# LSTM recurrence with a filled-in second layer: ScalarE's filler work by a budget, x's clamp on VectorE, the output sum through PSUM

## Chip, cores and metric

One core of a Trainium2 chip. The metric is the device time of one execution in microseconds, the median of several runs. Every engine (TensorE or PE, VectorE or DVE, ScalarE or ACT, GpSimd or POOL, SyncE or SP) works through its own queue in order; semaphores order them among each other.

## The reference

`x` has 8 sequences of 512 steps with 512 features, `cond` is 8 x 512. Two residual layers follow each other.

```python
# layer 1: an LSTM, hidden size 512, started from cond
a = x_t @ Wx + b + h @ Wh                  # 2048 columns
i, f, o = sigmoid(a[:, :1536]) in thirds;  g = tanh(a[:, 1536:])
c = f * c + i * g;   h = o * tanh(c)
x = x + h                                  # for all t
# layer 2: a causal convolution over 8 taps (cond holds the taps), then a scan over 64 states
conv = conv_b + sum_k x_pad[:, k:k+512] * cond[k]
proj = conv @ Wp + bp                      # 128 columns
B = softplus(proj[:, :64]);  C = tanh(proj[:, 64:]);  u = x @ Ws + bs
s = decay * s + dt * B * u;  y = C * s
x = x + y @ Wo + bo
```

All in fp32 at the interface.

## The kernel before

The features lie on the partitions in four chunks k = 0 to 3 of 128, time and batch on the free axis (8 batch columns per step). Layer 1 is a loop over 512 steps written out in full. Layer 2 is cut into blocks of 32 steps (256 columns), at the end into 32, 16, 8 and 8; its work is put into the gaps of the loop as *filler*.

**One recurrent step.** The hidden units are worked in two halves, A and B, each with its own PSUM tiles. Both matrices are held as a high and a low fp16 part. Per step and half (letters are those of the string `ORDER`, lines those of the profile before):

- PE: `h_mm` (L317) multiplies the state `stat` of the step before into the PSUM tile `hp` of the half, in the order A0 A1 b0 A2 A3 B1 B2 B3 and at `H` the last 64 columns of half B; `x_mm` (L306) adds the input's product for a step pair ahead. PE needs the state of half A for chunks 0 and 1, of half B for 2 and 3.
- VectorE: `T` and `t` transpose `hp` (L577, L580), `a` adds the halves of the gates into `zp` (L584), `v` and `c` update the cell, `c` into `zp` columns 48 to 63 (L599, L603), `i`, `m` and `l` make the new state (L612, L615, L618).
- GpSimd: `b` (L589). ScalarE: `g`, `o`, `k` (L593, L596, L606) are the tanh's, `p` (L609) copies the cell, `y` (L673) preloads a PSUM tile with the bias, `q` (L668) is a small copy.

`zp` is a pair of PSUM tiles, one per half, 64 columns each.

**Filler.** `Filler` holds a list per kind of work, and `pop` takes the head of a list if its dependencies were done at least a step (`gap`) before. While the loop is written out, three places in each step take from these lists:

- at `H`, behind the last x matmuls of the step, PE takes from `pl2`, `pl` until a budget is used up (1 unit, from step 480 on 3; a matmul of 128 columns is a unit);
- at `f`, behind the last state update, VectorE takes from `xd`, `d2`, `dve` as long as the told costs fit into `FILL` = 0.8;
- at `E`, at the end of the step, ScalarE takes two entries from `xa`, `al2`, `al`, and GpSimd one from `po`.

An entry can be several instructions: `act1` is two ScalarE instructions (L515, L516), `act2` four (the three of `softplus_act`, L206 to L208, and L520). What is left when the loop ends is drained list by list; that is the tail. Before it stand 14 dummy matmuls (L622).

**The filler by line.** For the input of layer 1 (`add_x`, per block and chunk): clamp on GpSimd (L441), fp16 high part on ScalarE (L444), low part on VectorE (L446). For a block of layer 2 (`add_l1`): the copy of the 7 steps before the block (L471, ScalarE); x + h per chunk (L476, VectorE); convolution, first tap on ScalarE (L493), seven on VectorE (L488); the matmul for u (L500) and ScalarE's bias (L502); the projection (L509); `act1`, `act2`; on VectorE softplus (L212 to L218), dt * B * u (L531), carry (L533), scan (L535), carry out (L537), C * s (L538); the output matmul of each chunk (L544) into a bank of `fps`, and VectorE's sum of it with the bias and x (L548), then the store. In the last three blocks one to four chunks of the convolution go to PE (`wpj`, L509).

The PSUM tiles are `hpb` (four of 512 columns), `fps` (two of 512) and the two `zp`.

Of the kernel before, what the change touches and what calls it, by code (L numbers as in the profile page):

```python
# [9 lines left out]
F32 = mybir.dt.float32  # L10
I32 = mybir.dt.int32
AF = mybir.ActivationFunctionType
# [14 lines left out]
DUMMY = 4  # L27
FILL = 0.8
TAILD = 14
LN2 = 0.6931471805599453  # L30
# [4 lines left out]
class Filler:  # L35
# [5 lines left out]
    def __init__(self, banks):  # L41
        self.q = {q: [] for q in ("po", "xa", "xd", "pl2", "d2", "al2", "pl", "dve", "al", "sp")}
        self.done = {}
        self.n = 0
        self.banks = banks
        self.free = {i: -10 for i in range(len(banks))}
# [34 lines left out]

    def drain(self, engs=("po", "xa", "xd", "al2", "d2", "d2", "d2", "pl2", "pl2", "pl", "pl", "dve", "al", "sp"),
              upto=None):

        def more(e):
            return self.q[e] and (upto is None or self.q[e][0][0] <= upto)
        while any([more(e) and self._try(e, None) for e in engs]):
            pass
# [3 lines left out]
def lstm_conv_ssm_kernel(ctx: ExitStack, tc: tile.TileContext, xT, condT, wx, wh, brow, cbp, wpp, bpp,  # L92
# [5 lines left out]
    l1blocks = [(i * BLK, BLK, 0) for i in range(NBLK - 2)]  # L98
    l1blocks += [(T - 64, 32, 0), (T - 32, 16, 4), (T - 16, 8, 4), (T - 8, 8, 2)]
    v, s, pe, sp = nc.vector, nc.scalar, nc.tensor, nc.sync  # L100
# [66 lines left out]

    zp = [pp.tile([128, 64], F32, name=f"zp{i}") for i in range(2)]
    fps = [pp.tile([128, 2 * NT], F32, name=f"fps{i}") for i in range(2)]
# [34 lines left out]
    def softplus_act(a, e, x):  # L204

        s.activation(e, a, AF.Exp, scale=-1.0)  # L206
        s.activation(a, a, AF.Tanh, scale=0.5, bias=hln2[0:64])
        s.activation(x, a, AF.Square, scale=-0.5, bias=half[0:64])  # L208

# [17 lines left out]
    s.activation(sp2[0], al2, AF.Abs)  # L227
    softplus_act(*sp2[0:3])
    dt = sp2[3][:, 1:2]
# [136 lines left out]


    bsum = [cp.tile([128, 256], F32, name=f"bsum{h}") for h in range(2)]
    run(*first[:4])
# [56 lines left out]
    for k in range(4):  # L426
        last = fl.add("pl", lambda k=k: pe.matmul(bk0["b"][:, 0:1], wp[:, k], cb[:, k:k + 1], start=k == 0, stop=k == 3),
                      take=bk0 if k == 0 else None)
    fl.add("al", lambda: s.activation(bpc, bk0["b"][:, 0:1], AF.Identity, bias=bp), deps=(last,), gap=0, give=bk0)
    for k in range(4):  # L430
        for j in range(8):
            fl.add("al", lambda k=k, j=j: s.activation(wpj[:, j, k], wp[:, k], AF.Copy, scale=cond[:, k, j:j + 1]))

# [3 lines left out]
    def add_x(n, t0=0, after=-1):  # L437
        for k in range(4):
            src, tmp, dst = x_parts(n, k, t0)
            sx = SX[:, k:k + 1]  # L440
            a = fl.add("po", lambda k=k, src=src, tmp=tmp: nc.gpsimd.tensor_scalar(  # L441
                tmp, src, CL[:, 0, k:k + 1], CL[:, 1, k:k + 1], op0=ALU.min, op1=ALU.max),
                deps=(xlast.get((n - 1, k)),), after=after)
            a = fl.add("xa", lambda sx=sx, tmp=tmp, dst=dst: s.activation(dst[0], tmp, AF.Copy, scale=sx),  # L444
                       deps=(a,), after=after)
            xlast[n, k] = fl.add("xd", lambda sx=sx, tmp=tmp, dst=dst: v.scalar_tensor_tensor(  # L446
                dst[1], tmp, sx, dst[0], op0=ALU.mult, op1=ALU.subtract), deps=(a,), after=after, cost=0.4)
# [4 lines left out]
    def add_l1(i, t0, L, pk):  # L452
# [11 lines left out]
        unit, cost = max(N / 128, 1), N / 1000 + 0.14  # L464
        kk = 1

# [3 lines left out]
        if i:  # L470
            halo = fl.add("al", lambda: s.activation(X[:, :, 0:H0], Xp[:, :, Lp * NB:Lp * NB + H0], AF.Copy),  # L471
                          deps=(p1["x2"], free), after=A)
        x2 = []
        for k in range(0, 4, kk):
            def f(k=k):
                v.scalar_tensor_tensor(X[:, k:k + kk, H0:H0 + N],  # L476
                                       hb[n % 2][:, k:k + kk, r0:r0 + L, :].rearrange("p k t b -> p k (t b)"), 0.5,
                                       xbuf[n % 4][:, k:k + kk, r0 * NB:r0 * NB + N], op0=ALU.mult, op1=ALU.add)
            x2 += [fl.add("dve", f, deps=(free,), after=A, cost=kk * cost)] * kk
        me["x2"] = x2[-1]  # L480

        cvd = {}
        for j in range(8):
            for k in range(pk, 4):
                def f(k=k, j=j):
                    src = X[:, k, j * NB:j * NB + N]
                    if j:
                        v.scalar_tensor_tensor(cv[:, k, 0:N], src, cond[:, k, j:j + 1], cv[:, k, 0:N],  # L488
                                               op0=ALU.mult, op1=ALU.add)
                    elif pk:  # L490
                        s.activation(cv[:, k, 0:N], src, AF.Copy, scale=cond[:, k, 0:1])  # L491
                    else:
                        s.activation(cv[:, k, 0:N], src, AF.Identity, bias=cb[:, k:k + 1], scale=cond[:, k, 0:1])  # L493
                deps = (halo, x2[k], p1.get("proj")) if j == 0 else (cvd[k],) if j == 1 else ()
                cvd[k] = fl.add("dve" if j else "al", f, after=A, deps=deps, cost=cost)

        bk = {}
        for k in range(4):
            def f(k=k, bk=bk):
                pe.matmul(bk["b"][0:64, 0:N], ws[:, k], X[:, k, H0:H0 + N], start=k == 0, stop=k == 3)  # L500
            last = fl.add("pl", f, deps=(x2[k], p2.get("u")), after=A, take=bk if k == 0 else None, cost=unit)
        fl.add("al", lambda bk=bk: s.activation(u[:, 0:N], bk["b"][0:64, 0:N], AF.Identity, bias=bs),  # L502
               deps=(last,), gap=0, give=bk)
        bk = {}
# [8 lines left out]

        def act1(bk=bk):
            s.activation(ab[:, 0:N], bk["b"][0:64, 0:N], AF.Abs, bias=b[0:64])  # L515
            s.activation(rl[:, 0:N], bk["b"][0:64, 0:N], AF.Relu, bias=b[0:64])  # L516

        def act2(bk=bk):
            softplus_act(ab[:, 0:N], e[:, 0:N], x[:, 0:N])
            s.activation(C[:, 0:N], bk["b"][64:128, 0:N], AF.Tanh, bias=b[64:128])  # L520
        last = fl.add("al2", act1, deps=(last, p2.get("wo")), gap=0)
        last = fl.add("al2", act2, deps=(last, p1.get("y")), give=bk)
        for f in softplus_dve(ab[:, 0:N], e[:, 0:N], x[:, 0:N], rl[:, 0:N], w[:, 0:N]):
            fl.add("d2", f, deps=(last,), cost=cost)

# [3 lines left out]
        def bt(a):  # L529
            return a[:, 0:N].rearrange("p (b t) -> p t b", b=NB)  # L530
        me["u"] = fl.add("d2", lambda: v.scalar_tensor_tensor(bt(e), tb(rl), dt, tb(u), op0=ALU.mult, op1=ALU.mult),  # L531
                         cost=cost)
        fl.add("d2", lambda: v.scalar_tensor_tensor(bt(e)[:, 0], carry, dec, bt(e)[:, 0],  # L533
                                                    op0=ALU.mult, op1=ALU.add), cost=0.18)
        fl.add("d2", lambda: v.tensor_tensor_scan(w[:, 0:N], dect[L].rearrange("p b t -> p (b t)"), e[:, 0:N], 0.0,  # L535
                                                  op0=ALU.mult, op1=ALU.add), cost=1.6 * cost)
        fl.add("d2", lambda: v.tensor_copy(carry, bt(w)[:, L - 1]), cost=0.1)  # L537
        me["y"] = y = fl.add("d2", lambda: v.tensor_tensor(tb(C), tb(C), bt(w), op=ALU.mult), cost=1.3 * cost)  # L538
        kb = min(2 * NT // N, 4)
        for k0 in range(0, 4, kb):  # L540
            bk = {}
            for k in range(k0, k0 + kb):
                def f(k=k, bk=bk):
                    pe.matmul(bk["b"][:, k % kb * N:k % kb * N + N], wo[:, k], C[:, 0:N], start=True, stop=True)  # L544
                me["wo"] = last = fl.add("pl2", f, deps=(y,), take=None if k % kb else bk, cost=unit)
            for k in range(k0, k0 + kb):
                def g(k=k, bk=bk):
                    v.scalar_tensor_tensor(o[:, k, 0:N], bk["b"][:, k % kb * N:k % kb * N + N], bo[:, k:k + 1],  # L548
                                           X[:, k, H0:H0 + N], op0=ALU.add, op1=ALU.add)
                me["out"] = fl.add("d2", g, deps=(last,), gap=0, give=bk if k == k0 + kb - 1 else None, cost=cost)  # L550
        fl.add("sp", lambda: sp.dma_start(outT[:, :, t0:t0 + L, :].rearrange("p k t b -> p k (t b)"), o[:, :, 0:N]),
# [76 lines left out]
    for t in range(T):  # L628
# [17 lines left out]
        for op in ORDER.split():  # L646
# [11 lines left out]
            elif op == "f":  # L658
                left = FILL
                while True:  # L660
                    got = fl.pop("xd", t, left) or fl.pop("d2", t, left) or fl.pop("dve", t, left)
                    left -= got
                    if not got:
                        break
# [17 lines left out]
            elif op == "E":  # L682
                for _ in range(2):
                    fl.pop("xa", t) or fl.pop("al2", t) or fl.pop("al", t)
                fl.pop("po", t)
            else:
                getattr(ch[op[1]], "o_" if op[0] == "o" else op[0])()
# [5 lines left out]

    fl.drain(("al2", "d2", "d2", "d2", "pl", "pl", "dve", "al"))
    fl.drain()
# [62 lines left out]
```

## Time and profile before

| | us |
|---|---|
| runs (3) | 1887.14 to 1888.98, median 1888.84 |
| profiled execution | 1887.91 |
| its span on the core | 1886.1 |
| first L577 of step 0, from the span's start | 42.41 |
| first L577 of step 511 | 1848.68 |
| VectorE busy | 1661.7 (88%) |
| PE busy | 1614.8 (86%) |
| ScalarE busy | 913.4 (48%) |

Granted clock of PE over the span: 0.992.

Rows of the operations that the change touches, mean of one in ns (busiest shape):

| line | engine | shape | count | mean |
|---|---|---|---|---|
| L441 clamp | POOL | 128x256 | 60 | 592 |
| L444 high part | ACT | 128x256 | 60 | 500 |
| L446 low part | DVE | 128x256 | 60 | 476 |
| L493 first tap | ACT | 128x256 | 60 | 589 |
| L488 other taps | DVE | 128x256 | 420 | 477 |
| L476 x + h | DVE | 128x256 | 60 | 417 |
| L548 last sum | DVE | 128x256 | 60 | 474 |
| L544 output matmul | PE | 64x256 | 120 records, two a matmul | 425 |
| L673 bias into PSUM | ACT | 128x256 | 508 | 383 |

How to read the views: in the timeline a row is start, duration (both us), engine, line, operation, out<-in, and in brackets the idle time of the engine before it with what ended it; neighbours of a kind are merged. In the waits a row is who waited for whom, the sum in us, how often, and the longest.

### The profile page before, as it was taken

What the parts mean: (1) busy time and instruction counts of PE and PEld (TensorE: products, weight loads), DVE (VectorE), ACT (ScalarE), POOL (GpSimd) and SP (SyncE); (2) the same over time, 40 slices, a digit from 0 to 9 for tenths busy, and PEclk for the clock granted to TensorE, in tenths of its full rate; (3) what the DMA queues carried; (4) which work ended last, traced back from release to release, by engine and by line L of the source; (5) the groups of instructions that cost most, each with busy time, mean ns of one, the idle gap of its engine ahead of it and who ended that gap; (6) DMA issues with size and microseconds to landing.
All of it is one profiled execution on the core that took longest, in us unless ns stands there. A gap on an engine that the chain in (4) does not pass through costs nothing.

```text
span 1886.1 us, 123963 instructions
## 1 busy us (share of the span) xinstructions
PE 1614.8 (86%) x53917; PEld 1313.1 (70%) x53917; DVE 1661.7 (88%) x9392; ACT 913.4 (48%) x5194; POOL 316.0 (17%) x1366
## 2 busy tenths in 40 slices
PE   5878888888888889888888988889888888988897
PEld 4666676677677677776776767767766767767686
DVE  8878889898998989889898998989899898998985
ACT  5555444454544545444454544445444454544442
POOL 1211111111211111111121111111111121111110
PEclk8999999999999999999999999999999999999997
DMA  6000000000000000000000000000000000000000
GB/s 238 5 4 15 4 27 4 4 27 4 27 4 4 27 4 27 4 27 4 4 27 4 26 5 4 27 5 27 4 27 5 4 15 4 16 4 15 5 5 23
DMA packets 21444, 33.78 MB, mean 18 GB/s; under 512 B 2592, under 2 KB 19616, under 8 KB 19872
## 3 DMA queue, kind: packets, MB, share of 16 engines
q1 hardware_dynamic: 20656, 25.71, 4.0%
q8 instruction: 421, 6.90, 1.5%
q14 instruction: 127, 1.04, 0.2%
q10 hardware_dynamic: 240, 0.13, 0.0%
HBM read 17.45 MB, written 8.39 MB: 14 GB/s over the span
## 4 chain that ended last, share of the span: by engine, by line
DVE 67%; PE 16%; ACT 7%; issue 4%; POOL 4%; DMA 1%; SPq 0%; DVEq 0%; ACTq 0%
DVE Z L577 18%; PE hp L317 13%; DVE Zo L580 9%; DVE wraw L488 9%; DVE zp L584 8%; DVE stat L618 4%; POOL zo L589 4%; DVE stat L612 4%; ACT gate L596 4%; DVE u L599 3%; DVE zp L603 3%; DVE hb L615 3%; ACT tc L606 2%; DMA x<-in_xT_dram 1%; PE fps L509 1%
## 5 line engine op out<-in xcount | busy, mean ns | idle before, releaser
L317 PE MATMUL hp<-whh,stat 128*16 128x256 f16 x18428 | 1017.8, 262 | 239.9 <-DVE stat L618 225.9
L317 PEld LDWEIGHTS <-stat 128*16 128x16 f16 x36856 | 860.0, 92 | 486.7 <-DVE stat L618 408.6
L317 PE MATMUL hp<-whl,stat 128*16 128x256 f16 x18428 | 1013.3, 261 | 0.2 <-DVE whl L281 0.2
L593 ACT ACTIVATE gate<-zp 128x48 f32<-128x48 f32 x1022 | 214.8, 210 | 781.5 <-DVE zp L584 778.9
L306 PE MATMUL hp<-wxh,xs 128*32 128x256 f16 x8192 | 518.4, 273 | 6.4 <-DVE xs L357 6.4
L306 PE MATMUL hp<-wxl,xs 128*32 128x256 f16 x8192 | 518.8, 273 | 0.0
L577 DVE STREAM_TRANSPOSE Z<-hp 128x192 f32<-128x192 f32 x1024 | 391.6, 382 | 102.0 <-PE hp L317 89.9
L589 POOL TENSOR_TENSOR zo<-Zo 128x16 f32<-128x16 f32 x1024 | 226.4, 221 | 1455.0 <-DVE Zo L580 1455.0
L306 PEld LDWEIGHTS <-xs 128*32 128x32 f16 x16384 | 403.5, 97 | 15.8 <-DVE xs L357 6.7
L596 ACT ACTIVATE gate<-zo 128x16 f32<-128x16 f32 x1022 | 220.9, 216 | 141.2 <-POOL zo L589 140.9
L612 DVE SCALAR_TENSOR_TENSOR stat<-gate,tc 128x16 f16<-128x16 f32 x1024 | 178.4, 174 | 68.5 <-ACT tc L606 0.2
L580 DVE STREAM_TRANSPOSE Zo<-hp 128x64 f32<-128x64 f32 x1024 | 233.3, 228 | 2.7
L584 DVE TENSOR_TENSOR zp<-Z 128x48 f32<-128x48 f32 x1024 | 211.6, 207 | 0.0
L618 DVE TENSOR_TENSOR stat<-hb,stat 128x16 f16<-128x16 f32 x1024 | 186.8, 182 | 17.5
L673 ACT ACTIVATE hp<-bsum 128x256 f32<-128x256 f32 x508 | 194.7, 383 | 0.0
L488 DVE SCALAR_TENSOR_TENSOR wraw<-x2b,cond,wraw 128x256 f32<-128x256 f32 (+1 forms) x434 | 188.5, 471 | 4.7 <-ACT wraw L491 4.7
L609 ACT ACTIVATE gate<-zp 128x16 f32<-128x16 f32 x1024 | 189.5, 185 | 0.0
L615 DVE SCALAR_TENSOR_TENSOR hb<-gate,tc 128x16 f32<-128x16 f32 x1024 | 187.2, 183 | 0.0
L606 ACT ACTIVATE tc<-zp 128x16 f32<-128x16 f32 x1024 | 185.0, 181 | 0.2 <-DVE zp L603 0.2
L599 DVE SCALAR_TENSOR_TENSOR u<-gate 128x32 f32<-128x32 f32 x1024 | 175.7, 172 | 4.5 <-ACT gate L593 3.7
L603 DVE SCALAR_TENSOR_TENSOR zp<-u 128x16 f32<-128x16 f32 x1024 | 177.4, 173 | 0.0
L681 POOL COPY seenp<-gate 128x1 f32<-128x1 f32 x256 | 46.9, 183 | 79.5 <-ACT gate L596 79.5
(125 smaller groups left out, 774.7 us busy)
## 6 DMA issues: line engine op xcount, KB each, us to landing
x<-in_xT_dram SPq DMA_DIRECT2D x15, 512.0 KB, 4.0
out_dram<-wraw SPq DMA_DIRECT2D x15, 512.0 KB, 3.6
wraw<-in_wh_dram SPq DMA_DIRECT2D x4, 1024.0 KB, 14.4
wraw<-in_wx_dram SPq DMA_DIRECT2D x4, 1024.0 KB, 11.2
x<-in_xT_dram SPq DMA_DIRECT2D x2, 256.0 KB, 13.3
wp<-in_wp_dram SPq DMA_DIRECT2D x1, 256.0 KB, 7.0
out_dram<-wraw SPq DMA_DIRECT2D x1, 256.0 KB, 2.8
out_dram<-wraw SPq DMA_DIRECT2D x2, 128.0 KB, 2.2
```

The costliest lines, as they stand in the source:

```text
L306: pe.matmul(hp[h][P % 2][32 * q:32 * q + 32, :], S[:, k, P % (BLK // 2)], W[:, k, q, 256 * h:256 * h + 256], start=False, stop=False, tile ...
L317: pe.matmul(hp[h][(t // 2) % 2][32 * q:32 * q + o + 16, a], S[:, k, 0:o + 16], wb[0][p][:, k, q, 256 * h + a.start:256 * h + a.stop], star ...
L488: v.scalar_tensor_tensor(cv[:, k, 0:N], src, cond[:, k, j:j + 1], cv[:, k, 0:N], op0=ALU.mult, op1=ALU.add)
L577: v.transpose(self.Z.rearrange("p g r -> p (g r)"), self.P[:, 0:192])
L580: v.transpose(self.Zo.rearrange("p g r -> p (g r)"), self.P[:, 192:256])
L584: v.tensor_tensor(self.zp[:, 0:48].rearrange("p (g b) -> p g b", b=8), self.Z[:, :, o:o + 8], self.Z[:, :, o + 8:o + 16], op=ALU.add)
L589: pool.tensor_tensor(self.zo.rearrange("p (g b) -> p g b", b=8), self.Zo[:, :, o:o + 8], self.Zo[:, :, o + 8:o + 16], op=ALU.add)
L596: s.activation(self.G[:, 48:64], self.zo, AF.Tanh, scale=self.inv)
L603: v.scalar_tensor_tensor(self.zp[:, 48:64], self.u[:, 1], 0.5, self.u[:, 0], op0=ALU.mult, op1=ALU.add)
L612: v.scalar_tensor_tensor(self.S[:, :, 0:8], r8(self.G[:, 48:64]), 1.0, r8(self.tc), op0=ALU.add, op1=ALU.mult)
L615: v.scalar_tensor_tensor(self.hf, r8(self.G[:, 48:64]), 1.0, r8(self.tc), op0=ALU.add, op1=ALU.mult)
L618: v.tensor_tensor(self.S[:, :, 8:16], self.hf, self.S[:, :, 0:8], op=ALU.subtract)
```

## The change

- Clamp of x: from GpSimd (`po`) to VectorE (`xc`), taken at `f`.
- x + h of a block: a list of its own (`x2`), which `f` asks before the clamp and before layer 2's other VectorE work.
- ScalarE at `E`: no longer two entries, but as many as fit by their told costs into `FILLA` = 1.0. `act1` and `act2` are split into single instructions (the tanh of C now third), each with a cost. GpSimd gets no filler any more.
- The told costs of VectorE's strided or scanned pieces are raised (1.7 and 1.6 times `cost`), that of the first softplus piece is lowered.
- For blocks of 32 steps the output no longer goes through `fps`. The two `zp` tiles become 512 columns wide, the recurrence keeps columns 0 to 63, and columns 64 to 319 are `ops`. ScalarE writes x + bias there (L561), PE adds the output product (L566, accumulating), ScalarE copies the sum to SBUF (L572). All on the list `ao`, two chunks at a time. The shorter blocks keep the old way (L550, L554).
- Two matmuls of 512 columns in the prologue write both `zp` banks once.
- The block of steps 448 to 479 takes one chunk of its convolution on PE.

In the changed kernel the recurrence's L584, L603, L618 are L607, L626, L641.

```diff
+FILLA = 1.0
...
-    l1blocks += [(T - 64, 32, 0), (T - 32, 16, 4), (T - 16, 8, 4), (T - 8, 8, 2)]
+    l1blocks += [(T - 64, 32, 1), (T - 32, 16, 4), (T - 16, 8, 4), (T - 8, 8, 2)]
...
-    zp = [pp.tile([128, 64], F32, name=f"zp{i}") for i in range(2)]
+    zps = [pp.tile([128, 512], F32, name=f"zp{i}") for i in range(2)]
+    zp = [t[:, 0:64] for t in zps]
+    ops = [t[:, 64:64 + NT] for t in zps]
...
+    for b_ in zps:
+        pe.matmul(b_, ident, x2b[0].rearrange("p k n -> p (k n)")[:, 0:512], start=True, stop=True)
...
-            a = fl.add("po", lambda k=k, src=src, tmp=tmp: nc.gpsimd.tensor_scalar(
+            a = fl.add("xc", lambda k=k, src=src, tmp=tmp: v.tensor_scalar(
                 tmp, src, CL[:, 0, k:k + 1], CL[:, 1, k:k + 1], op0=ALU.min, op1=ALU.max),
-                deps=(xlast.get((n - 1, k)),), after=after)
+                deps=(xlast.get((n - 1, k)),), after=after, cost=0.27)
...
+        acost = N / 1000 + 0.24
...
-            x2 += [fl.add("dve", f, deps=(free,), after=A, cost=kk * cost)] * kk
+            x2 += [fl.add("x2", f, deps=(free,), after=A, cost=cost + 0.06)]
...
-        last = fl.add("al2", act1, deps=(last, p2.get("wo")), gap=0)
-        last = fl.add("al2", act2, deps=(last, p1.get("y")), give=bk)
-        for f in softplus_dve(ab[:, 0:N], e[:, 0:N], x[:, 0:N], rl[:, 0:N], w[:, 0:N]):
-            fl.add("d2", f, deps=(last,), cost=cost)
+        acts = [lambda bk=bk: s.activation(ab[:, 0:N], bk["b"][0:64, 0:N], AF.Abs, bias=b[0:64]),
+                lambda bk=bk: s.activation(rl[:, 0:N], bk["b"][0:64, 0:N], AF.Relu, bias=b[0:64]),
+                lambda bk=bk: s.activation(C[:, 0:N], bk["b"][64:128, 0:N], AF.Tanh, bias=b[64:128])]
+        acts += softplus_act(ab[:, 0:N], e[:, 0:N], x[:, 0:N])
+        for m, f in enumerate(acts):
+            last = fl.add("al2", f, deps=(last, (p2.get("wo"), None, None, p1.get("y"), None, None)[m]), gap=0,
+                          give=bk if m == 2 else None, cost=acost)
...
+            for k in range(k0, k0 + kb):
+                def g(k=k, bk=bk):
+                    s.activation(ops[k % 2], X[:, k, H0:H0 + N], AF.Identity,
+                                 bias=bo[:, k:k + 1])
+                pre = fl.add("ao", g, deps=(me.get("out", p1.get("out")), x2[k]), after=A, cost=acost)
             for k in range(k0, k0 + kb):
                 def f(k=k, bk=bk):
-                    pe.matmul(bk["b"][:, k % kb * N:k % kb * N + N], wo[:, k], C[:, 0:N], start=True, stop=True)
-                me["wo"] = last = fl.add("pl2", f, deps=(y,), take=None if k % kb else bk, cost=unit)
+                    pe.matmul(ops[k % 2], wo[:, k], C[:, 0:N], start=False,
+                              stop=False, skip_group_check=True)
+                me["wo"] = last = fl.add("pl2", f, deps=(y, pre), gap=1, cost=unit)
+
             for k in range(k0, k0 + kb):
-                def g(k=k, bk=bk):
-                    v.scalar_tensor_tensor(o[:, k, 0:N], bk["b"][:, k % kb * N:k % kb * N + N], bo[:, k:k + 1],
-                                           X[:, k, H0:H0 + N], op0=ALU.add, op1=ALU.add)
-                me["out"] = fl.add("d2", g, deps=(last,), gap=0, give=bk if k == k0 + kb - 1 else None, cost=cost)
+                def h(k=k):
+                    s.activation(o[:, k, 0:N], ops[k % 2], AF.Copy)
+                me["out"] = fl.add("ao", h, deps=(last,), cost=acost)
...
-                    got = fl.pop("xd", t, left) or fl.pop("d2", t, left) or fl.pop("dve", t, left)
+                    got = (fl.pop("xd", t, left) or fl.pop("x2", t, left) or fl.pop("xc", t, left) or fl.pop("d2", t, left)
+                           or fl.pop("dve", t, left))
...
-                for _ in range(2):
-                    fl.pop("xa", t) or fl.pop("al2", t) or fl.pop("al", t)
-                fl.pop("po", t)
+                left = FILLA
+                while True:
+                    got = fl.pop("xa", t, left) or fl.pop("ao", t, left) or fl.pop("al2", t, left) or fl.pop("al", t, left)
+                    left -= got
+                    if not got:
+                        break
```

## The prediction

> **What bounds the kernel now.** I read the page first (shares and chain), then the timeline of a plain recurrence step and of one with a filler that hurts, then the waits, then the timeline of the tail.
>
> ```profile
> PE 1614.8 (86%) x53917; PEld 1313.1 (70%) x53917; DVE 1661.7 (88%) x9392; ACT 913.4 (48%) x5194; POOL 316.0 (17%) x1366
> DVE 67%; PE 16%; ACT 7%; issue 4%; POOL 4%; DMA 1%; SPq 0%; DVEq 0%; ACTq 0%
> ```
>
> No engine is full; a chain that runs once per step through PE, VectorE and ScalarE sets the pace. The timeline shows one plain step (first transpose L577 at 1059.26, next at 1062.76) and most of the next one:
>
> ```profile
> 1059.26 0.38 DVE L577 STREAM_TRANSPOSE Z<-hp 128x192 f32<-128x192 f32 x1
> ...
> 1060.33 0.22 DVE L584 TENSOR_TENSOR zp<-Z 128x48 f32<-128x48 f32 x1
> ...
> 1060.46 0.18 DVE L603 SCALAR_TENSOR_TENSOR zp<-u 128x16 f32<-128x16 f32 x1
> ...
> 1060.73 0.70 PE L544 MATMUL fps<-wraw,wo 64*128 64x256 f32 x2
> ...
> 1061.25 0.17 DVE L618 TENSOR_TENSOR stat<-hb,stat 128x16 f16<-128x16 f32 x1
> ...
> 1062.76 0.38 DVE L577 STREAM_TRANSPOSE Z<-hp 128x192 f32<-128x192 f32 x1
> ...
> 1065.17 0.59 POOL L441 TENSOR_SCALAR xc<-x,cl 128x256 f32<-128x256 f32 x1
> ...
> 1065.36 0.42 DVE L618 TENSOR_TENSOR stat<-hb,stat 128x16 f16<-128x16 f32 x1
> ```
>
> Call the start of the first L577 of a step 0. Half B's gate sum L584 starts at 1.07, half A's cell update L603 at 1.20, and a filler matmul of the output projection (L544) runs on PE from 1.47 to 2.17, after all recurrent work of PE in that step and before the next. L618 of half A starts at 1.99 and frees PE for the next step; 3.50 after the start comes the next L577. So the stretch from 1.07 to 1.99 on VectorE is on the chain with no slack, and L544 beside it costs nothing: nobody in that stretch waits for it.
>
> From the starts of the first L577 (42.41 for step 0, 1848.68 for step 511) 511 intervals make 1806.27 us. Steps with nothing but recurrence, and most with two fillers, take 3.498. The excess over that is 1806.27 - 511 x 3.498 = 18.8 us. It is 14.0 in blocks 1 to 14 (1.0 each), 1.3 in the first 32 steps and 3.4 in the last 31. Inside a block it sits in few steps: four with a clamp on POOL (L618 takes 0.42 instead of 0.17 while L441 runs, as shown; +0.25, +0.06, +0.25, +0.06), the one behind the four-in-one ScalarE piece (+0.29), and one with L218 and L531 together on VectorE, 1.09 us (+0.15, 0.09 given back).
>
> **The parts, costed.**
>
> *Clamp to VectorE, ScalarE by budget.* 64 POOL clamps go; 64 VectorE ones come. Nearest rows: L212, the same kind of operation on 64 rows by 256, 0.277 us; POOL's own 0.592. I take 0.28. In the built order each stands with L476 (0.417) or L446 (0.476): 0.70 to 0.76. Two L488 (0.477 each, 0.95) fit today at 3.498, so this hides. At 0.592 it would make 1.07 and cost about 0.15 in four steps per block, 9 us. ScalarE gets at most two long pieces per step or three of 0.393, 1.18 us at the dearest. Today a pair of L493 (0.589 each) starts at 1065.48 and ends 1066.56, 0.06 after the next L577 and 0.37 before the L584 starts whose output ScalarE needs first, so these hide; without that cover each tenth over 0.37 would be a tenth on the step. The POOL, four-in-one and L531 excesses go: the 14.0 us, and about 1.0 of the first block. In the last 31 steps the excess comes from two or three PE fillers in one step (two of 256 columns +0.31, three of 128 columns +0.12). The built order has 5 and 7 such steps there, 2.4 in place of 3.4. **Gain: 14.0 + 1.0 + 1.0 = 16.0 us.**
>
> *Last sum through PSUM.* 60 L548 (0.474) leave VectorE's fillers, worth nothing on the chain; 60 + 60 ScalarE pieces come. Their bounds are L673 (0.383, into PSUM) and L493 (0.589, with a bias); even two at 0.589 hide as above. The matter is where the sums live: in columns 64 to 319 of the same two tiles whose columns 0 to 63 are zp, the recurrence's own buffers. The waits of the built program follow the tile, not the columns. All 56 matmuls (L566) that stand inside the loop keep L544's place on PE, behind the last x matmul of the step, and VectorE's next write of that half's zp waits for the matmul: for half A that is the cell update (L603, now L626), for half B the gate sum (L584, now L607). Both stand ahead of everything else VectorE has in the step.
>
> The price, from the shown rows: PE ends at 2.17, and VectorE starts 0.04 after PE's end (in the tail PE ends L544 at 1876.40, L548 starts at 1876.44), so at 2.21. Half B: 2.21 - 1.07 = 1.14 late. Half A: 2.21 - 1.20 = 1.01 late. Everything to L618 queues behind; PE waits for L618; so the whole step grows by it. 26 steps of each: 26 x 2.15 = 55.9. Two more steps hold two L566 each; two L544 in one step took 1.13 us, so half B's sum starts at 1.47 + 1.13 + 0.04 = 2.64, 1.57 late: 3.1. **Cost: 59.0 us.** Bounds per wait: 0.8, if VectorE's pieces close up behind it, to 1.3, if the second wait that the instruction now carries and the restart add 0.15; 45 to 73 in all.
>
> Could such a wait be empty, because the columns differ? The waits of the kernel before show the same kind biting: PE's matmul into the last 64 columns of a half's hp tile waits for the transpose that reads the first 192.
>
> ```profile
> PE hp L317 <- DVE Z L577: 1.0, 2, 0.5
> ```
>
> The Trainium skill, PSUM — Partial Sum Buffer, "PSUM bank collisions raise a hardware error", goes further: accesses are to be guarded by bank and quadrant, never by address. By that rule every L566 has to wait for zp's users and they for it, and the sum keeps the 59.0; by columns alone it would be nil. No run here shows such a collision.
>
> *The start.* Two matmuls of 512 columns on fp32 now stand on PE between L327 (9.85 + 0.37) and L339 (10.95). L292's 256 columns take 12.05/48 = 0.25 per record, two records a matmul: 0.5, so 1.0 for 512 columns, 2.0 for both. L339 then starts near 12.2 rather than 10.95. Behind it are the bias matmuls, ScalarE's bsum and its first L276, from which ScalarE and VectorE run chained to step 0. **Cost 1.2 us** (0 to 1.5).
>
> *The tail.* VectorE's and ScalarE's second-layer work now comes later in a block, and the end feels it.
>
> ```profile
> 1851.09 0.35 ACT L515 ACTIVATE wraw<-fps,bpc 64x128 f32<-64x128 f32 x1
> ...
> 1853.20 7.36 PE L509 MATMUL fps<-x2b,wraw 128*128 128x64 f32 x64
> ...
> 1868.52 0.31 ACT L515 ACTIVATE wraw<-fps,bpc 64x64 f32<-64x64 f32 x1 [5.62 <-PE fps L509]
> ...
> 1882.04 0.86 DVE L548 SCALAR_TENSOR_TENSOR wraw<-fps,bo,x2b 128x64 f32<-128x64 f32 x4 [2.06 <-PE fps L544]
> ```
>
> From the last step's L577 (1848.68) the first of these is at +2.4 and the end of the last at +34.2. In the built order ten of the 32 projection matmuls of the 16-step block are left behind the dummies: 2.4 + 1.7 + 10 x 0.29 = +7.0 for its first activation. The next block's 32 matmuls need a bank that ScalarE frees at +8.1, and end at 8.1 + 7.4 = +15.5 (now +11.9). Then four L566 with a hand-over to ScalarE and back between pairs (about 3.1) and the 16-step block's four (2.0): +20.6. The last block's projection is split around the output matmuls of the block before it; these wait for that block's y. VectorE turns to it when the 16-step block's sums (1.2) and the last ScalarE piece behind them are through, near +22.5, and needs 3.3 for eleven pieces and the convolution pieces between: +25.8. Then two outputs 1.0, two projections 0.5, two outputs 1.0, nine 2.1 and two 1.0 on PE: +31.4. Behind that, as now: six activations 1.6, VectorE's eleven pieces 2.8, four matmuls 2.0, four sums 0.9, 0.1 of hand-overs = +38.8. **Cost 4.6 us** (2 to 8).
>
> *Sum.* 59.0 - 16.0 + 1.2 + 4.6 = +48.8 on the profiled execution's 1887.91 (span 1886.1 and 1.8 around it): 1936.7. The median of the runs is 0.9 above that execution, so **1937.6**.
>
> **Rivals.**
> 1. The waits don't bite: L566 is done before VectorE comes to zp. Then the gain stands alone, 1888.8 - 16.0 + 5.8 = 1878.6, faster. It needs L566 to end before 1.07, against 2.17 in the trace; the break-even is (16.0 - 5.8)/56 = 0.18 us per wait. For it speaks only that ends of matmuls are modelled; but L548's start behind L544 fits them within 0.04. 5%.
> 2. Only one half's waits reach the end, say because half A's delay is taken up by pieces that otherwise wait for half B: 1937.6 - 26 x 1.01 = 1911. Against it: L618 of half A itself lies behind L603. 6%.
> 3. ScalarE's new pieces come late as well: L584 of half A also waits for ScalarE's last access to zp in four steps per block. If that ended 0.2 after 0.43, 56 x 0.2 = 11 more: 1949. By the rows it ends 0.4 or more before. 9%.
>
> **How the numbers follow.** The forecast has 80%. Its own bounds are 1937.6 - 14 - 3 to 1937.6 + 14 + 3, and up to 9 more for a dear clamp; rival 3 lies inside, rival 2 outside. 1919 to 1955 should hold 8 in 10. A difference under 0.2% (3.8 us) can't be told from none here. Faster 0.05 (rival 1), same 0.01, slower 0.94.
>
> **What would show it.** Right: steps 14, 15, 18 and 19 of a block at 4.5 to 4.7 us with VectorE idle about 1 us, released by PE's L566; all other steps of blocks 1 to 14 at 3.50; L618 nowhere at 0.42; first L577 near 43.6; last span after it near 42. Wrong: these four steps at 3.5, or VectorE idle before other work than L607 and L626.

## The result, and the profile after

The changed kernel takes **1939.88 us** (median of 4 runs, 1939.44 to 1940.68) against 1888.64 for the kernel before on the same chip: ratio 1.0277, 95% interval 1.0264 to 1.029. It is slower by 2.8%. The profiled execution took 1939.63, its span is 1937.9.

In the changed kernel the lines that the prediction speaks of are L600 (first transpose), L607 (gate sum), L626 (cell update), L641 (state, low part), L566 (output matmul into `ops`), L561 and L572 (ScalarE before and behind it), L448 (clamp) and L373 (the two initial matmuls). From the page, busy times and the chain that ended last:

```profile
PE 1615.7 (83%) x53935; PEld 1318.0 (68%) x53935; DVE 1656.2 (85%) x9389; ACT 954.4 (49%) x5313; POOL 281.8 (15%) x1302
DVE 62%; PE 26%; ACT 5%; issue 4%; POOL 3%; DVEq 0%; POOLq 0%; ACTq 0%
```

PE has 1 us more work than before and VectorE 5.5 us less, yet the span is 51.7 longer: the chain's share moved from VectorE (67 to 62%) to PE (16 to 26%). The timeline shows two neighbouring steps of a block; the columns are start, duration, instruction, and in brackets the idle time before it and what ended that.

```profile
1015.72 0.38 DVE L600 STREAM_TRANSPOSE Z<-hp 128x192 f32<-128x192 f32 x1 [0.21 <-PE hp L321]
...
1017.19 0.70 PE L566 MATMUL zp<-wraw,wo 64*128 64x256 f32 x2
1017.93 0.18 DVE L626 SCALAR_TENSOR_TENSOR zp<-u 128x16 f32<-128x16 f32 x1 [0.92 <-PE zp L566]
...
1018.68 0.17 DVE L641 TENSOR_TENSOR stat<-hb,stat 128x16 f16<-128x16 f32 x1
...
1020.19 0.38 DVE L600 STREAM_TRANSPOSE Z<-hp 128x192 f32<-128x192 f32 x1
...
1021.67 0.70 PE L566 MATMUL zp<-wraw,wo 64*128 64x256 f32 x2
1022.41 0.22 DVE L607 TENSOR_TENSOR zp<-Z 128x48 f32<-128x48 f32 x1 [1.11 <-PE zp L566]
...
1023.32 0.17 DVE L641 TENSOR_TENSOR stat<-hb,stat 128x16 f16<-128x16 f32 x1
...
1024.82 0.38 DVE L600 STREAM_TRANSPOSE Z<-hp 128x192 f32<-128x192 f32 x1
```

The first step is 1020.19 - 1015.72 = 4.47 long, the second 1024.82 - 1020.19 = 4.63, where a plain step takes 3.498. In both the matmul keeps its old place (it starts 1.47 and 1.48 after the step's start and takes 0.70), and VectorE stands idle 0.92 and 1.11 before the very instructions that write that half's zp. L641 of half A comes 2.96 and 3.13 after the step's start instead of 1.99. The waits (engine and line that waited, what it waited for: us in total, times, longest) count them:

```profile
DVE zp L607 <- PE zp L566: 31.7, 28, 1.5
DVE zp L626 <- PE zp L566: 23.8, 26, 0.9
ACT tc L629 <- DVE zp L626: 22.3, 26, 0.9
```

In the kernel before, VectorE's writes of zp wait for no matmul. All kernels below are taken apart in the same way: the start of step 0 (first transpose), the 511 intervals between first transposes, their excess over 511 x 3.498, and the rest of the span (tail). "With" are the steps in which an output matmul into `ops` starts. All from the profiled executions, in us.

| kernel | start | 511 steps | excess | of it with / without | tail | span |
|---|---|---|---|---|---|---|
| before | 42.4 | 1806.3 | 18.8 | | 37.5 | 1886.1 |
| after | 44.9 | 1849.9 | 62.4 | 58.2 / 4.3 | 43.0 | 1937.9 |
| e1_old_sum | 42.0 | 1792.6 | 5.1 | | 50.3 | 1884.9 |
| e2_only_sum | 44.8 | 1868.2 | 80.7 | 61.8 / 18.9 | 47.1 | 1960.0 |
| e4_late_one_tile | 44.9 | 1799.9 | 12.4 | 8.1 / 4.3 | 47.0 | 1891.7 |
| e5_init_late | 42.0 | 1850.4 | 62.9 | | 42.7 | 1935.0 |
| e6_one_chunk_pe | 42.3 | 1794.7 | 7.2 | | 43.5 | 1880.5 |
| e7_own_bank | 42.3 | 1791.8 | 4.4 | 0.7 / 3.6 | 55.3 | 1889.5 |
| e8_pool_clamp | 41.5 | 1803.6 | 16.1 | | 49.4 | 1894.5 |
| e9_bank_chunk | 42.3 | 1792.0 | 4.6 | | 49.6 | 1883.9 |
| e10_last_old | 42.3 | 1792.5 | 5.1 | | 34.4 | 1869.2 |

The runs of e2, e7 and e9 fall in two groups 6 to 8 us apart, and their profiled executions (1961.78, 1891.28 and 1885.71) are of the longer group, so that their spans here are 5 to 7 us longer than their median run's.

### The profile page after: what moved, and what is told of

It is laid out like the page before. It is cut to its first block, busy times and chain, and to the rows that moved or that the text cites. A ratio compares the mean times of both kernels' runs of the same rounds, so it can differ in the third digit from the quotient of the medians.

```text
span 1937.9 us, 124180 instructions
## 1 busy us (share of the span) xinstructions
PE 1615.7 (83%) x53935; PEld 1318.0 (68%) x53935; DVE 1656.2 (85%) x9389; ACT 954.4 (49%) x5313; POOL 281.8 (15%) x1302
## 4 chain that ended last, share of the span: by engine, by line
DVE 62%; PE 26%; ACT 5%; issue 4%; POOL 3%; DVEq 0%; POOLq 0%; ACTq 0%
PE hp L321 19%; DVE Z L600 17%; DVE Zo L603 8%; DVE zp L607 7%; DVE wraw L495 6%; DVE stat L641 4%; DVE zp L626 4%; DVE stat L635 3%; DVE u L622 3%; POOL zo L612 3%; PE hp L310 3%; ACT gate L619 3%; DVE hb L638 3%; PE zp L566 2%; ACT tc L629 1%
## 5 line engine op out<-in xcount | busy, mean ns | idle before, releaser
L600 DVE STREAM_TRANSPOSE Z<-hp 128x192 f32<-128x192 f32 x1024 | 392.4, 383 | 101.1 <-PE hp L321 88.1
L607 DVE TENSOR_TENSOR zp<-Z 128x48 f32<-128x48 f32 x1024 | 212.5, 207 | 31.7 <-PE zp L566 31.7
L603 DVE STREAM_TRANSPOSE Zo<-hp 128x64 f32<-128x64 f32 x1024 | 233.3, 228 | 2.1
L626 DVE SCALAR_TENSOR_TENSOR zp<-u 128x16 f32<-128x16 f32 x1024 | 177.3, 173 | 23.8 <-PE zp L566 23.8
L641 DVE TENSOR_TENSOR stat<-hb,stat 128x16 f16<-128x16 f32 x1024 | 179.0, 175 | 17.5
L495 DVE SCALAR_TENSOR_TENSOR wraw<-x2b,cond,wraw 128x256 f32<-128x256 f32 (+1 forms) x427 | 184.8, 471 | 0.0
```

The costliest lines, as they stand in the source:

```text
L600: v.transpose(self.Z.rearrange("p g r -> p (g r)"), self.P[:, 0:192])
L603: v.transpose(self.Zo.rearrange("p g r -> p (g r)"), self.P[:, 192:256])
L607: v.tensor_tensor(self.zp[:, 0:48].rearrange("p (g b) -> p g b", b=8), self.Z[:, :, o:o + 8], self.Z[:, :, o + 8:o + 16], op=ALU.add)
L626: v.scalar_tensor_tensor(self.zp[:, 48:64], self.u[:, 1], 0.5, self.u[:, 0], op0=ALU.mult, op1=ALU.add)
L641: v.tensor_tensor(self.S[:, :, 8:16], self.hf, self.S[:, :, 0:8], op=ALU.subtract)
```

## The experiments

The theory: the output matmuls cost their time because their sums stand in the same PSUM tiles as zp, so that VectorE's writes of zp wait for them. Rivals: ScalarE's new pieces cost it, or VectorE's longer list; and the 14 to 16 us that the other parts should bring could be an error.

**e1_old_sum**: the changed kernel with the last sum as before (matmul into a filler bank, sum by VectorE).

```diff
-    zps = [pp.tile([128, 512], F32, name=f"zp{i}") for i in range(2)]
-    zp = [t[:, 0:64] for t in zps]
-    ops = [t[:, 64:64 + NT] for t in zps]
+    zp = [pp.tile([128, 64], F32, name=f"zp{i}") for i in range(2)]
...
-                pre = fl.add("ao", g, deps=(me.get("out", p1.get("out")), x2[k]), after=A, cost=acost)
...
-                    pe.matmul(ops[k % 2], wo[:, k], C[:, 0:N], start=False,
-                              stop=False, skip_group_check=True)
+                    pe.matmul(bk["b"][:, k % kb * N:k % kb * N + N], wo[:, k], C[:, 0:N], start=True, stop=True)
...
-                    s.activation(o[:, k, 0:N], ops[k % 2], AF.Copy)
+                    v.scalar_tensor_tensor(o[:, k, 0:N], bk["b"][:, k % kb * N:k % kb * N + N], bo[:, k:k + 1],
+                                           X[:, k, H0:H0 + N], op0=ALU.add, op1=ALU.add)
```

> The changed kernel with the last sum put back: output matmul into fps, VectorE's sum of PSUM, bias and x, zp 64 columns wide, no matmuls of 512 columns in the prologue. Clamp on VectorE, budget for ScalarE, single pieces and told costs stay. Theory (the loss is VectorE waiting for the output matmul on a shared zp tile): 57.8 us of waits and 2.5 us of the start go, so about 1878 to 1880, faster than both kernels; all steps of blocks 1 to 14 at 3.50; first L577 near 42.4. Rival (the reordered filler or ScalarE's new load costs the time): over 1925.

Measured 1886.2, ratio 0.9991 (0.9982 to 1.0001): no difference that can be told. The loop did what was expected, 13.7 shorter than before. The tail took it back: 50.3 against 37.5, with 80 VectorE instructions behind the last step's own instead of 66, and 34.7 us of PE work from that step on instead of 23.8. The clamps and the higher told costs fill VectorE's places (in most blocks of 32 steps only 2 stay empty instead of 5), so the second layer's work falls behind and is done when nothing hides it. An expectation that counted only the loop missed by 7.

**e2_only_sum**: the other half, the kernel before with only the sum through PSUM (the same tiles, L561, L566 and L572, list `ao`; clamp on GpSimd, ScalarE's old rule of two entries).

> The kernel before with the last sum through PSUM alone: wide zp tiles, ScalarE's two pieces per chunk on a list that the old two-entries rule serves, the two matmuls in the prologue; clamp stays on GpSimd. Theory: 1888.6 + 57.8 of waits + 2.5 at the start + 0 to 2 in the tail = 1949 to 1951, with four steps per block about 1 us longer. Rival (the waits matter only together with the new order): under 1910.

Measured 1957.13 (1953.89 to 1961.78), ratio 1.0372 (1.0351 to 1.0393). The loop is 61.9 longer than before: the sum alone costs about what the forecast charged for it, and the loops of the two halves of the change (-13.7 and +61.9) add up to the whole's +43.6 within 5 us. The total is 6 above the expectation: in the profile the tail is 9.6 longer than before's, where 0 to 2 was expected, and this execution is 4.7 over the median.

**e4_late_one_tile**: the changed kernel, but all sums in half A's tile alone, one chunk at a time, and the matmul issued behind half A's cell copy (`p`) rather than at `H`.

```diff
-    ops = [t[:, 64:64 + NT] for t in zps]
+    ops = [zps[0][:, 64:64 + NT]] * 2
...
-        kb = min(2 * NT // N, 4)
+        kb = min(2 * NT // N, 4) if L < BLK else 1
...
+                while op == "pA" and late and room > 0:
+                    cost = fl.pop("pl2", t) or fl.pop("pl", t)
```

> The changed kernel with all output sums in half A's zp tile, one chunk at a time, and the output matmul issued behind half A's last use of zp in the step (ScalarE's copy of the cell) instead of ahead of its cell update. The number of matmuls and of ScalarE's pieces is the same; VectorE then no longer waits for the matmul, but the matmul waits for ScalarE's copy, which ends about 1.70 after the step's start, and ends near 2.44, 0.24 after PE could start the next step. Theory: 56 x 0.24 = 13 in place of 57.8: about 1895. Rival (the matmul into the bank or ScalarE's traffic slows the step by itself): stays near 1940.

Measured 1893.32, ratio 1.0028 (1.0018 to 1.0039). The 56 steps with an output matmul hold 8.1 of excess instead of 58.2: with the same number of matmuls and of ScalarE pieces, most of the loss goes when the matmul takes the tile at another moment (the choice of the tile and the one chunk at a time changed with it). The wait is still in the trace, turned round: PE now waits for ScalarE's last access to the tile, and little stands behind PE there. From the waits of this kernel (its L574 is the output matmul, L640 the copy `p`):

```profile
PEld zp L574 <- ACT gate L640: 26.8, 56, 0.5
```

The expectation had put 0.24 a step on it, 13 in all.

**e5_init_late**: the changed kernel with the two initial matmuls behind the warm-up, ahead of `bias_mm(0, h)`.

> The changed kernel with the two 512-column matmuls of the prologue moved behind the warm-up matmuls, ahead of the bias of the first step, where PE idles 6 us. Theory (they hold up the bias matmuls, ScalarE's first weight part and with it the whole chained prologue): first L577 near 42.4 instead of 44.9, time about 1937.4. Rival (something else moved the start): 1939.9.

Measured 1937.43, ratio to before 1.0267 (1.0252 to 1.0283). Step 0 starts at 41.98 instead of 44.94: the early place of two matmuls cost 3 us. The timelines of the changed kernel and of e5 show the same four records:

```profile
10.03 3.62 PE L373 MATMUL zp<-x2b,ident 128*128 128x512 f32 x4
```

```profile
29.13 1.88 PE L415 MATMUL zp<-x2b,ident 128*128 128x512 f32 x4
```

That is 0.905 us for each record at 10 us and 0.47 at 29 us (a matmul is two records).

**e7_own_bank**: the run that decides between the tile and rival A. All parts of the change, all ScalarE pieces and all output matmuls stay, but the sums stand in one of the two filler banks, which the second layer gives up until the last 32-step block is out. The one initial matmul is placed as in e5.

```diff
-    zps = [pp.tile([128, 512], F32, name=f"zp{i}") for i in range(2)]
-    zp = [t[:, 0:64] for t in zps]
-    ops = [t[:, 64:64 + NT] for t in zps]
+    zp = [pp.tile([128, 64], F32, name=f"zp{i}") for i in range(2)]
+    ops = [fps[1][:, NT * i:NT * i + NT] for i in range(2)]
...
     fl = Filler(fps)
+    del fl.free[1]
...
-                me["out"] = fl.add("ao", h, deps=(last,), cost=acost)
+                me["out"] = fl.add("ao", h, deps=(last,), cost=acost,
+                                   give={"i": 1} if k == 3 and i == NBLK - 2 else None)
```

> The changed kernel with all of its parts, the last sum through PSUM by ScalarE included, but the sums stand in one of the two banks that the second layer's matmuls used (fps[1]) instead of in columns 64 to 319 of the two zp tiles; the second layer has the other bank alone until the last long block is out, and zp is a tile of 64 columns again. The same L566-type matmuls, the same ScalarE pieces, one initial matmul of 512 columns instead of two, behind the warm-up. Theory (what costs is the shared tile: VectorE's writes of zp wait for the output matmul): no step over 4 us is left, the excess over 3.498 per step falls from 62.4 us to 4 to 7, first step-T at 42, tail 43 to 45 (one bank less), so 1880 to 1883 us, faster than both kernels. Rival A (the cost is ScalarE's 120 extra pieces or the matmuls that accumulate onto what ScalarE wrote, wherever they are): the long steps stay, excess 50 to 65, 1935 to 1942. Rival B (one bank is too little for the second layer): steps stay at 3.50 but the work piles up, tail over 55, 1892 or more.

Measured 1884.87, ratio 0.9984 (0.9973 to 0.9995). The long steps are gone. In blocks 2 to 14 the same 52 steps hold 0.1 of excess, where they held 55.0. Timeline of one such step (its L565 is the output matmul; the next step starts at 882.63, 3.50 later):

```profile
879.13 0.38 DVE L600 STREAM_TRANSPOSE Z<-hp 128x192 f32<-128x192 f32 x1
...
880.21 0.22 DVE L607 TENSOR_TENSOR zp<-Z 128x48 f32<-128x48 f32 x1
880.33 0.18 DVE L626 SCALAR_TENSOR_TENSOR zp<-u 128x16 f32<-128x16 f32 x1
...
880.61 0.70 PE L565 MATMUL fps<-wraw,wo 64*128 64x256 f32 x2
...
881.13 0.17 DVE L641 TENSOR_TENSOR stat<-hb,stat 128x16 f16<-128x16 f32 x1
```

The matmul starts 1.48 after the step's start, as ever; L607 and L626 have not waited, and L641 stands at 2.00. So the shared tile is the cost, shown with everything else in place; ScalarE's pieces (rival A) are not. The sums here left the tile and the PSUM bank at once; no run keeps them in the bank under a tile of their own. The total missed the expected 1880 to 1883 by 2, and in the tail (55.3, or about 49 if the median run's 6 us less lie there, where 43 to 45 was expected). A reason can be read from the order of the program, which e10 tests below: with one bank the sixteen-step block's projection stands behind the long block's, and four output matmuls change hands with ScalarE twice.

**e6_one_chunk_pe**: e1 with one of the convolution's four channel chunks on PE in all 32-step blocks, to test whether the tail is VectorE's overflow (work that found no filler place in the steps).

```diff
-    l1blocks = [(i * BLK, BLK, 0) for i in range(NBLK - 2)]
+    l1blocks = [(i * BLK, BLK, 1) for i in range(NBLK - 2)]
```

> The kernel of e1 (changed kernel with the last sum back on VectorE), and in all 32-step blocks one of the four channel chunks of the convolution is done by PE (eight accumulated matmuls with scaled weights) instead of seven VectorE pieces, as the change does for the last 32-step block alone. Theory (e1's tail of 50.3 is VectorE's filler work that no longer fits into the steps: 75 VectorE instructions stand behind the last step, before 54): with 3.3 us less of it per block 66 are left, and by the slope of the runs so far, 0.6 us for each, the tail is 44 to 46; loop as e1, 1792 to 1794; 1880 to 1883. Rival (the tail is set by PE's chain of projections, not by VectorE's amount): tail stays at 49 to 51, 1885 to 1887.

Measured 1883.53, ratio 0.9966 (0.9953 to 0.9978). The tail fell from 50.3 to 43.5 with ten VectorE instructions fewer behind the last step (70 for 80; the expectation's counts of 75 and 54 for e1 and the kernel before are 80 and 66 in the traces). So less VectorE work per block shortens the tail, as expected; the loop took 2 back. But PE's work from the last step on fell too, from 34.7 to 28.8 us, and the tail goes with that more closely: in all eleven profiles the tail less PE's busy time in it is 11.7 to 15.7, the tail less VectorE's 17.5 to 37.2. This points to overflow on VectorE holding up PE's projections until nothing hides them. Here both fell at once; e10 below parts them.

**e9_bank_chunk**: e7 and e6 together.

> Both edits together on the changed kernel: sums in a bank of their own and one convolution chunk on PE in all 32-step blocks. If the shared tile is the cost and VectorE's amount sets the tail: first step-T 42, loop 1792 to 1794, 60 VectorE instructions behind the last step and a tail of 40 to 42; 1876 to 1880, the fastest. If ScalarE's pieces are the cost: 1930 or more. If one bank is too little: over 1885.

Measured 1879.2, ratio 0.9952 (0.9937 to 0.9967), within the expected range. The tail is 49.6 in the profile, or about 43 if the median run's 6 us less lie there; 40 to 42 was expected.

**e8_pool_clamp**: e1 with the clamp back on GpSimd.

> The kernel of e1 with x's clamp back on GpSimd: what is left of the change is ScalarE's budget and the new told costs. It prices the clamp against the budget within e1's gain of 13.7 in the loop. Theory (four GpSimd clamps per block lengthen two steps by 0.25 and two by 0.06, as in the trace of before): loop 9 to 10 longer than e1's 1792.6, L618's kind back at 0.42 beside the clamp, tail as e1 (50), 1894 to 1897. Rival (the clamp is worth little, the budget is what gains): loop within 3 of e1's, 1886 to 1889.

Measured 1896.62, ratio 1.0036 (1.0024 to 1.0049). The loop is 10.9 longer than e1's: of the 13.7 that the parts without the sum bring in the loop, the clamp's move is 10.9, and the rest (ScalarE's budget, the new told costs, the order of the lists, the one chunk on PE) 2.7. The answers for one line (the state's low part: least, median and longest ns) show the way it works, first e1, then e8:

```profile
L619 DVE TENSOR_TENSOR stat<-hb,stat x1024: 174/175/177, 44.2 to 1837.2; 128x16 f16<-128x16 f32 x171
```

```profile
L619 DVE TENSOR_TENSOR stat<-hb,stat x1024: 163/175/421, 43.9 to 1847.7; 128x16 f16<-128x16 f32 x171
```

With the clamp on GpSimd the instruction on the chain takes up to 421 ns, without it never over 177.

**e10_last_old**: e9 with the last 32-step block's sum in the old way, so that both banks are back for the end.

```diff
-            if L < BLK:
+            if i > NBLK - 3:
...
-                                   give={"i": 1} if k == 3 and i == NBLK - 2 else None)
+                                   give={"i": 1} if k == 3 and i == NBLK - 3 else None)
```

> The kernel of e9 (sums in a bank of their own, one convolution chunk on PE in all 32-step blocks) with the last 32-step block's sum done in the old way (matmul into a second-layer bank, sum by VectorE), so that the second layer has both banks again from 64 steps before the end. Nothing changes in the loop up to there: first step-T 42.3, loop 1791 to 1793. If the tail of e9 (49.6 in its profile, about 43 in most of its runs) is made by one bank and by the hand-overs between PE and ScalarE for the last long block's four sums, then 51 VectorE instructions are left behind the last step instead of 60, all sixteen-step projections are done ahead of the 14 dummies, and the tail is 36 to 39: 1872 to 1876, the fastest of all. Rival (the tail is set by the PE clock, which the profiles grant at 0.50 from 9 to 16 us after the last step, whatever is queued): 42 or more, 1879 or more.

Measured **1871.07** (1870.98 to 1871.1), ratio 0.9905 (0.9888 to 0.9921): faster than both kernels, and 2 below where the tail was put. Page and timeline of its end (L520 is the projection's activation, L515 the projection matmul, L553 the last sum of a short block):

```profile
PE 1671.8 (89%) x54129; PEld 1342.2 (72%) x54129; DVE 1618.8 (87%) x9295; ACT 937.8 (50%) x5291; POOL 281.4 (15%) x1302
```

```profile
1837.31 0.36 ACT L520 ACTIVATE wraw<-fps,bpc 64x128 f32<-64x128 f32 x1
...
1839.81 7.36 PE L515 MATMUL fps<-x2b,wraw 128*128 128x64 f32 x64 [0.40 <-ACT wraw L508]
...
1865.13 0.86 DVE L553 SCALAR_TENSOR_TENSOR wraw<-fps,bo,x2b 128x64 f32<-128x64 f32 x4 [2.12 <-PE fps L549]
```

VectorE has 37 us less to do than in the changed kernel and PE 56 more, and the loop is still as short as e1's (1792.5): PE's filler place had room for it. From the last step on, e10 and e9 have the same 66 VectorE instructions behind the step's own (not the 51 and 60 of the expectation), so it is not VectorE's amount that made e10's tail shorter. PE's busy time there fell from 36.6 to 21.3 us. Part of that is the granted clock, which in e9's profile falls 9 us behind the last step's transpose and in e10's 22 (last section). The first activation of the sixteen-step block stands 2.5 behind the last step's first transpose, as before the change (2.4).

## Why the prediction was right

1937.6 was forecast, 1939.88 measured; the span grew by 51.7, the sum had said 48.8. Term by term:

| term | forecast | measured |
|---|---|---|
| waits on the shared tile | +59.0 | +58.2 |
| gain in the loop | -16.0 | -14.5 |
| start | +1.2 | +2.5 |
| tail | +4.6 | +5.6 |

**The waits.** In both singles the working held: half A's steps are 0.97 longer (forecast 1.01; one of the 26 is 1.20), half B's 1.13 (1.14), the two double steps 1.56 and 1.57 (1.57), and e7 shows the reason. The idle time stands before L626 and L607, as named. The steps named (14, 15, 18 and 19 of a block) are the right ones in blocks 6 to 14; in blocks 2 to 5 they come one to four steps earlier. The rule of the Trainium skill, PSUM — Partial Sum Buffer, "PSUM bank collisions raise a hardware error", that accesses are to be guarded by bank and quadrant and not by address, fits this: zp's columns and the sums never overlap, and the built waits bite all the same until the sums stand in another bank. The collision itself, which the rule is there to prevent, no run shows.

**The gain.** Blocks 1 to 14 keep 1.3 of their 14.0 outside the steps with L566, and the last 31 steps keep 2.7 instead of 2.4; the first block gave 1.1 (forecast 1.0). The clamp was mis-sized: 0.28 was taken from a 64x256 operation, and L448 takes 0.41. It made no difference, as the pair with L483 or L453 (0.39 or 0.48) stays under the 0.95 that hides; of the steps with a clamp in blocks 1 to 14 only step 35, with L453 and L448 on VectorE and L451 and L500 on ScalarE, is 0.08 too long. Most of the 1.3 is one step per block with two convolution taps (L495), 0.08 each.

**The start.** The order of events was right, the size half: a matmul of 512 columns took 1.81, where 1.0 was worked out from L292's mean of 0.25 per record of 256 columns, a mean over 48 records of which nearly all run later and faster (last section). The forecast's own bound of 1.5 was too low.

**The tail.** 5.6 within 2 to 8. The steps were in the forecast's order: the first activation at +6.2 (forecast +7.0), the end of the next block's 32 matmuls (64 records) at +14.6 (+15.5), the last block's activation at +32.1 (+31.4). From the timeline, with the last step's L600 at 1894.83:

```profile
1901.06 0.36 ACT L521 ACTIVATE wraw<-fps,bpc 64x128 f32<-64x128 f32 x1 [3.71 <-PE fps L516]
...
1902.03 7.36 PE L516 MATMUL fps<-x2b,wraw 128*128 128x64 f32 x64 [0.40 <-ACT wraw L509]
...
1926.97 0.31 ACT L521 ACTIVATE wraw<-fps,bpc 64x64 f32<-64x64 f32 x1 [10.70 <-PE fps L516]
```

**The rivals.** The waits bite (1 falls); they bite for both halves (2 falls); ScalarE's pieces are not late (3 falls: in the waits no write of zp by VectorE waits for ScalarE, and all steps without an output matmul hold 4.3 together). The errors of the four terms are -0.8, +1.5, +1.3 and +1.0, 3.0 together; the medians show 2.3 of it. That the forecast is so near rests on the waits, the largest term by far and the best sized.

What the forecast did not see is why the change's good half cannot pay alone: its 13.7 in the loop come back as 12.9 in the tail when the sum stays on VectorE (e1). The tail was costed for this change only, and there the sum's move off VectorE hid part of the overflow (70 VectorE instructions behind the last step against e1's 80).

## What to carry to other kernels

Before a buffer gets a second user, look at who waits for its first user, and where in the chain: a matmul that was free on PE cost 1.0 to 1.1 us each once a recurrence's next write waited for it, and nothing in a bank of its own. Work that is moved onto an engine whose filler places are nearly full comes out at the end of the program, there and on the engines that wait for it; count what is left behind the loop on each engine, not only the steps. If two parts of a change have opposite signs, run each alone: here the clamp (e1 against e8) and the sum's idea (e10 against e6, ratios 0.9905 and 0.9966) were both worth keeping, and the place of the sums was wrong.

## What the runs showed of the hardware

PE ran at half its later rate at its first work: in e5 the same four records take 1.88 us at 29 us, in the changed kernel 3.62 at 10 us. Behind them, records of L296 (256 columns) start about 0.43 apart up to 18.22 and 0.22 apart from 18.53 on. The views give a granted clock of 1.00 there all the same: the trace's first clock record is at 18.41, and a stretch without a record is counted as full. In the eleven traces the first record comes 4.1 to 8.5 us behind PE's first matmul, 8.5 in the changed kernel, where PE is never idle in between. The Trainium skill, TensorE: Matmul & The Clock Gate, "Part 1: The HAM clock gate", says that the array runs at half clock until it has been busy for a window of some 3.4 us, and that the window runs freely. An estimate from this figure is 3.4 to 6.8 us, one window and up to one more for where it starts; five of the eleven traces lie above it.

At the end the granted clock falls to 0.50 in every kernel, and when it does differs: 16 to 22 us behind the last step's transpose in most, 9 to 10 in the profiles of e2, e7 and e9. In e7 it falls within the first microsecond of the 32 projection matmuls (64 records), which then take 13.13 us instead of 7.36. Timeline and windows of e7 (window, its length, busy time and instructions of PE, PEld, DVE, ACT and POOL, granted clock, DMA share, GB/s):

```profile
1843.62 13.13 PE L515 MATMUL fps<-x2b,wraw 128*128 128x64 f32 x64 [0.40 <-ACT wraw L508]
```

```profile
1842.00:1850.00 8.00, 7.06 (x42) 6.92 (x42) 3.53 (x14) 1.79 (x6) 0.00 (x0) 0.66 0.00 0
1850.00:1858.00 8.00, 8.00 (x35) 7.70 (x35) 0.00 (x0) 0.00 (x0) 0.00 (x0) 0.50 0.01 2
```

The mean of 0.66 over the first window puts the fall near 1844.5. The difference of 5.8 us is most of the 6 to 8 between the two groups of e7's runs. The shorter runs have no profile, but their granted clock over the span is 0.990 to 0.992, that of the longer ones 0.986 to 0.987. PE was busy for all of the second window and stayed at 0.50, so the same section's rule that a busy window of some 3.4 us brings the full clock does not hold for these 64-column fp32 matmuls. What sets the moment of the fall was not tried and stays open.
